# Second layer of a two-layer network: softplus pieces on ScalarE and direct products on VectorE stand at other steps

## The chip, the cores and the metric

The kernel runs on one core of one Trainium2 chip. Its engines are TensorE (PE; PEld is its weight load), VectorE (DVE), ScalarE (ACT), GpSimd (POOL) and SyncE (SP, which issues the DMAs). Each engine works through its own queue in order and waits for others through semaphores. The metric is device time in microseconds; before the change it is 8841.8 us, the median of three runs (8837.53 to 8855.01).

## The reference, cut to what matters

Everything is float32. The first layer is an attention block on 16 images of 128 channels and 56 x 56 pixels; the change leaves it alone. The second layer is a 3 x 3 convolution, a small state-space scan over 8 tokens, GroupNorm and a SiLU with residual:

```python
y = conv(x, conv_w) + conv_b
seq = y.reshape(B * H * W, 8, 16)                      # 8 tokens of 16 values a pixel
xi, z = split(seq @ in_proj_w.T)                       # 32 and 32
xc = silu(causal_conv1d(xi) + conv1d_b)
dt, Bm, Cm = split(xc @ x_proj_w.T, [1, 17])
dt = softplus(dt * dt_proj_w + dt_proj_b)
h = exp(dt * A) * h + dt * Bm * xc                     # for each of 8 tokens, 32 x 16 states
ym = (sum(h * Cm) + D * xc) * silu(z)
out = ym @ out_proj_w.T
return x + silu(groupnorm(out))
```

softplus(v) is computed as max(v, 0) + ln(1 + exp(-|v|)), with a correction of the rounding in 1 + e: u = (1 + e) - 1, and e - u is added to the logarithm.

## The kernel before, in words

The second layer (`layer1`) starts some 3250 us into the span. The work is cut into groups of 448 columns, 7 to an image, 112 in all. A group's scan runs in 14 steps, two a token (`jp` 0 and 1: each step takes half of the states, a tile of 128 x 896). The order of each engine's queue is written out by hand: the loop at the end of `layer1` runs over groups i and steps k, issues the scan's own instructions and then what `work(i, k)` lists for VectorE, TensorE and GpSimd (in this order). `_chain` keeps the recorded order on each engine. A list named `pe` holds steps that begin with a matmul, but what they issue on ScalarE goes into ScalarE's queue at the same place.

In each step k of group i stand, in this order:

- `advance` (VectorE): L946 multiplies the decay `a` (in PSUM, two buffers) by the state of the token before, L947 adds it to this token's input; for the last token, steps 12 and 13, L944 does it in one.
- `inject` (VectorE): L936 makes the input `h` of four steps later (at steps 10 to 13 that of the next group) from `x` (PSUM, one buffer) and the gate `bb`. The tiles `h` have four buffers; one that is written at step 12 for the next group was last read by GpSimd's weighing of token 5.
- `decay` (TensorE): L918 makes the exponent of step k + 2; `spread` (TensorE): L929 makes the `x` that L936 of step k + 1 reads.
- `decay_exp` (ScalarE): L921, the exponential of `a` in place, that L946 of step k + 2 reads.
- `weigh` (GpSimd, odd steps): L951 multiplies the states of a token by the gate `cb`.

`work(i, k)` adds the rest. For the next group (`nxt`) it prepares: `rate` (steps 1 and 2, one a half h): matmul L850 into bank `pq0`, then on ScalarE Abs L851 and Relu L852; `rate_exp`: L856 and L857 on ScalarE; `rate_log`: L861 and L862 on ScalarE; `rate_sum` (steps 6 and 8): L867 to L870 on GpSimd, which end with `dt` and `dtx`; `gate` (step 3): matmuls L876 into `pq0` and `pq1`, the copies L880 to `bs` and `cs` on ScalarE, and DMAs L882 to DRAM; `bring`: the loads of `bb` and `cb` from there; `inner(..., "zs", ...)` (step 4): matmuls L836, SiLU L837; `product` (step 10): L896 on GpSimd; `direct` (step 13): matmul L900 of that product into `pq0`. For the group after next, `sequences` (step 11: transposes L829 and copy L831) and `inner(..., "xc", ...)` (step 12). Each `inner` takes a ScalarE table load (L837), two SiLU, and a load back (L145): this is the SiLU burst that stands in steps 4 and 12.

For the group itself (`p`): `direct_mul`, L905 on VectorE, reads `pq0` that `direct` filled and `dtx`, and writes `ud`; `skip` (L966) and `gather` (L960, four matmuls) collect the token sums in `pq1`; `collect` (L973) adds `ud`; `gated` (L976) multiplies by `zs`; `project_out` (L994, with copies L1002, L1005 and L1007 on ScalarE) follows in steps 5 and 6 of the next group. The convolution of the next image (L787, into `pq0`) is spread over steps 5 to 10.

In the second group of an image the statistics of the image before are finished: L1027 with copy L1028, and L1038 with Ln L1039 and Exp L1040, through `pq0`. At step 12 of that group ScalarE also runs the normalising SiLU L1061 (`normalise`), two of 128 x 1568 with table loads, and GpSimd adds the residual (L1068) there and in the third group.

Of the kernel before, what the change touches and what calls it, by code (L numbers as in the profile page):

```python
# [711 lines left out]
def layer1(ctx: ExitStack, tc: tile.TileContext, x1, t, out):  # L712
# [45 lines left out]
    for w, name in ((wx, "b_kx"), (wv, "b_dtw")):  # L758
        k = w1.tile(list(w.shape), F32, tag="fold", name=name)
# [17 lines left out]
    def load_image(b):  # L777
        nc.sync.dma_start(pad[:, 1 : H + 1, 1 : W + 1], x1[b].rearrange("c (h w) -> c h w", w=W))
        tails[b] = w2.tile([P, 64], F32, tag="tail", name=f"tail_{b}")
# [104 lines left out]
    def bring(p, k, tokens):  # L884
        n = len(tokens)
        tile_ = w3.tile([P, 2, BLK], F32, tag="bc"[k] + "b", name=f"{'bc'[k]}b_{p['n']}_{tokens[0]}")
        src = p["dram", k][:, tokens[0] : tokens[0] + n, :].rearrange("s l n -> s (l n)")
        nc.sync.dma_start(
            tile_[:, 0:n, :].rearrange("p l n -> p (l n)"), src.unsqueeze(1).to_broadcast([16, 8, n * BLK])
        )  # L890
        for i, l in enumerate(tokens):
            p["gate", k, l] = tile_[:, i, :]
# [157 lines left out]
    def residual(b, k):  # L1050
        res = norms[b, k] = w1.tile([P, half], F32, tag="res", name=f"res_{b}_{k}")
        nc.sync.dma_start(res[0:64], x1[b][0:64, k * half : (k + 1) * half])
        if k == 0:
            nc.sync.dma_start(res[64:P], x1[b][64:P, 64 : half + 64])
        else:
            nc.sync.dma_start(res[64:P, 0 : half - 64], x1[b][64:P, half + 64 : HW])
            nc.sync.dma_start(res[64:P, half - 64 : half], x1[b][64:P, 0:64])
# [19 lines left out]
    def work(i, k):  # L1077


        def at(n):  # L1080
            return groups[n] if 0 <= n < len(groups) else None

        p, nxt, far, prev = at(i), at(i + 1), at(i + 2), at(i - 1)
        pe, dve, pool = [], [], []

        if prev:
            if k == 0:
                pe += [partial(gather, prev, 5), partial(gather, prev, 6)]
            if k == 1:
                pe.append(partial(gather, prev, 7))  # L1090
            if k == 3:
                dve.append(partial(collect, prev, 1))
            if k == 4:
                pool.append(partial(gated, prev, 1))
            if k in (5, 6):
                pe.append(partial(project_out, prev, k - 5))
            b = prev["b"]
            if prev["g"] % 2 and k in (9, 10):
                dve.append(partial(statistics, b, prev["g"] - 10 + k))
            if prev["g"] == NBLK - 1:  # L1100
                if k == 9:
                    dve.append(partial(statistics, b, NBLK - 1))
                if k == 12:
                    residual(b, 0)
        two = at(i - 2)
        if two and two["g"] == NBLK - 1:
            b = two["b"]
            if k == 3:
                pool.append(partial(deviation, b))
            if k == 5:  # L1110
                pe.insert(0, partial(group_var, b, 0))
            if k == 8:
                pool.append(partial(affine, b))
            if k == 12:
                pe += [partial(normalise, b, 0), partial(normalise, b, 1)]
            if k == 13:
                pool += [partial(store, b, 0, 0), partial(store, b, 0, 1), partial(residual, b, 1)]
        three = at(i - 3)
        if three and three["g"] == NBLK - 1 and k in (2, 4):
            pool.append(partial(store, three["b"], 1, k // 2 - 1))  # L1120

        if p:
            if k == 1:
                dve.append(partial(direct_mul, p))
            if k == 7:
                pe.append(partial(skip, p, 0))
            if k in (8, 9, 10):
                pe.append(partial(gather, p, k - 7))
            if k == 12:
                dve.append(partial(collect, p, 0))  # L1130
            if k == 13:
                pe += [partial(skip, p, 1), partial(gather, p, 4)]
                pool.append(partial(gated, p, 0))
            if k in (2, 6):
                bring(p, 0, {2: (4, 5), 6: (6,)}[k])
            if k in (1, 5, 9):
                bring(p, 1, {1: (3, 4), 5: (5, 6), 9: (7,)}[k])

        if nxt:
            if k in (1, 2):  # L1140
                pe.append(partial(rate, nxt, k - 1))
            if k in (2, 3):
                pe.append(partial(rate_exp, nxt, k - 2))
            if k in (3, 4):
                pe.append(partial(rate_log, nxt, k - 3))
            if k in (6, 8):
                pool.append(partial(rate_sum, nxt, k // 2 - 3))
            if k == 3:
                pe += [partial(gate, nxt, 0), partial(gate, nxt, 1)]
            if k == 4:  # L1150
                pe.insert(0, partial(inner, nxt, "zs", wz, w2, 0.0))
            if k == 7:
                bring(nxt, 0, (0, 1))
            if k == 8:
                bring(nxt, 1, (1, 2))
            if k == 11:
                bring(nxt, 0, (2, 3))
            if k == 10:
                pool.append(partial(product, nxt))
            if k == 13:  # L1160
                pe.append(partial(direct, nxt))

        if p and k in (5, 6, 7, 8, 9, 10) and p["b"] + 1 < NB:
            taps = {5: (0,), 6: (1,), 7: (2, 3), 8: (4, 5), 9: (6, 7), 10: (8,)}[k]
            pe.append(partial(convolve, p["b"] + 1, p["g"], taps))
        if p and p["g"] == NBLK - 1 and k == 11 and p["b"] + 2 < NB:
            load_image(p["b"] + 2)
        if two and two["g"] == NBLK - 1 and k == 2:
            pe.append(partial(group_mean, two["b"], 0))
        if far:  # L1170
            if k == 11:
                pe.append(partial(sequences, far))
            if k == 12:
                pe.insert(0, partial(inner, far, "xc", wx, w3, c1_b))
        return pe, dve, pool
# [16 lines left out]
    for i in range(-2, len(groups) + 3):  # L1192
        for k in range(14):
            now = 0 <= i < len(groups)
            if now:
                advance(*state_step(i, k))
            inputs = input_step(i, k + 4) if now or (i == -1 and k >= 10) else None
            if inputs:
                inject(*inputs)
            decays = state_step(i, k + 2) if now or (i == -1 and k >= 12) else None  # L1200
            if decays:
                decay(*decays)
            inputs = input_step(i, k + 5) if now or (i == -1 and k >= 9) else None
            if inputs:
                spread(*inputs)
            if decays:
                decay_exp(*decays)
            if now and k % 2:
                weigh(groups[i], 1 + k // 2)
            pe, dve, pool = work(i, k)  # L1210
            for part in (dve, pe, pool):
                for step in part:
                    step()
# [37 lines left out]
```

## Time and profile before

| | us |
|---|---|
| median of 3 runs | 8841.8 |
| the profiled execution, device time | 8843.74 |
| its span, first to last instruction | 8841.9 |
| L951 POOL, weigh, mean of 784 | 3.996 |
| L921 ACT, exponential, mean of 1568 | 0.900 |
| L936, L946, L947 DVE, means | 1.083, 1.091, 1.092 |
| L905 DVE, direct product, mean (4000 to 7000 us) | 0.676 |
| L856, L857, L861, L862 ACT, means (4000 to 7000 us) | 0.567, 0.578, 0.661, 0.561 |
| L837 and L145 ACT, table load | 1.283 |
| mean granted clock | 0.966 |

In the profile a line such as `6240.30 1.10 DVE L946 ... x1 [0.76 <-ACT a L921]` is read: at 6240.30 us of the span VectorE starts an instruction of line 946 that takes 1.10 us; before it the engine was idle for 0.76 us, and what ended the wait was ScalarE's line 921. A float32 matmul shows as several records (x2, x4, x8), and successive instructions of an engine overlap by some 0.1 us.

### The profile page before, as it was taken

To read this page: it belongs to the slowest core of one execution; us is meant where nothing else is said; L and a number is where in the kernel's file an instruction comes from. 1 tells how busy PE (TensorE), PEld (TensorE's weight loads), DVE (VectorE), ACT (ScalarE), POOL (GpSimd) and SP (SyncE) were. 2 spreads that over 40 slices of the span, in tenths; PEclk is the share of its full clock that TensorE was granted. 3 is DMA by queue.
4 is the path that set the end of the run, shared out by engine and by line. 5 is a ranking of instruction groups with operands and counts; after the bars stand their busy time and mean duration, and the time that the engine had idled before them with its cause. 6 is when DMAs were issued, how large, how long until landed. Compare 5 with 4: busy or idle time off the path is not lost.

```text
span 8841.9 us, 151450 instructions
## 1 busy us (share of the span) xinstructions
PE 8013.1 (91%) x52860; PEld 3322.9 (38%) x52860; DVE 7764.8 (88%) x10358; ACT 5603.8 (63%) x10516; POOL 7035.4 (80%) x5664
## 2 busy tenths in 40 slices
PE   6999999999999879999999999999999999999987
PEld 3444444444444433333333333333333333333332
DVE  7999999999999839898898988988988989889887
ACT  4776777777777636666655665665656665666654
POOL 5878888878888328888888888888888888888887
PEclk8999999999999989999999999999999999999997
DMA  2333333333333222333333333333333333333332
GB/s 62 85 85 89 87 87 87 86 87 89 87 86 88 76 61 80 93 90 83 90 90 83 91 83 99 84 88 93 87 85 86 88 92 91 82 98 85 87 89 69
DMA packets 764424, 757.86 MB, mean 86 GB/s; under 512 B 188688, under 2 KB 663952, under 8 KB 761616
## 3 DMA queue, kind: packets, MB, share of 16 engines
q1 hardware_dynamic: 763664, 748.18, 32.8%
q8 instruction: 422, 6.91, 0.3%
q14 instruction: 338, 2.77, 0.1%
HBM read 439.61 MB, written 102.76 MB: 61 GB/s over the span
## 4 chain that ended last, share of the span: by engine, by line
PE 31%; ACT 24%; DVE 21%; POOL 11%; issue 10%; DMA 1%; SPq 0%; ACTq 0%; POOLq 0%; DVEq 0%
PE pq L787 8%; PE a L918 8%; ACT a L921 5%; DVE a L946 5%; DVE lepe L460 4%; DVE h L947 4%; POOL xh L263 4%; PE pq L960 4%; POOL e L379 4%; PE x L929 3%; ACT L837 3%; DVE h L936 3%; POOL tap L261 2%; ACT L145 2%; DVE sst L363 2%
## 5 line engine op out<-in xcount | busy, mean ns | idle before, releaser
L951 POOL TENSOR_TENSOR cst<-h,cb 128x1792 f32<-128x1792 f32 x784 | 3129.4, 3996 | 855.1 <-DVE h L947 580.4
L921 ACT ACTIVATE a<-a 128x896 f32<-128x896 f32 x1568 | 1404.3, 900 | 1772.7 <-PE x L929 1174.8
L936 DVE TENSOR_TENSOR h<-x,bb 128x896 f32<-128x896 f32 x1568 | 1697.6, 1083 | 276.9 <-PE x L929 145.6
L918 PE MATMUL a<-dt,adec 32*128 32x448 f32 x6272 | 1659.7, 606 | 214.4 <-DVE h L947 213.5
L946 DVE TENSOR_TENSOR a<-a,h 128x896 f32<-128x896 f32 x1344 | 1466.3, 1091 | 358.1 <-ACT a L921 357.5
L460 DVE SCALAR_TENSOR_TENSOR lepe<-vpad,lep,lepe 128x448 f32<-128x448 f32 x2688 | 1718.4, 678 | 0.6
L929 PE MATMUL x<-dtx,amask 32*128 32x448 f32 x6272 | 1664.8, 608 | 25.5 <-DVE h L936 24.5
L947 DVE TENSOR_TENSOR h<-a,h 128x896 f32<-128x896 f32 x1344 | 1467.0, 1092 | 45.8
L379 POOL TENSOR_SCALAR e<-e,sst,zero 128x256 f32<-128x256 f32 x1568 | 861.6, 560 | 451.4 <-DVE sst L375 396.6
L369 ACT ACTIVATE e<-ps,sst 128x256 f32<-128x256 f32 x1568 | 728.8, 469 | 544.5 <-DVE sst L363 493.6
L787 PE MATMUL pq<-x1pad,conv 128*128 128x448 f32 x2016 | 942.8, 580 | 59.5 <-ACT gst L1039 32.5
L918 PEld LDWEIGHTS a<-dt,adec 32*128 32x128 f32 x6272 | 484.2, 188 | 1247.4 <-DVE h L947 578.4
L263 POOL TENSOR_TENSOR xh<-xh,tap 128x448 f32<-128x448 f32 x735 | 841.4, 1145 | 42.5
L960 PE MATMUL pq<-cst,sel 128*32 128x448 f32 x6272 | 750.9, 564 | 1.5 <-POOL cst L951 1.5
L401 PE MATMUL ptt<-ident,e 128*128 128x128 f32 x3136 | 546.4, 285 | 92.3 <-POOL e L379 75.2
L363 DVE TENSOR_REDUCE sst<-ps 128x2 f32<-128x512 f32 x784 | 540.4, 689 | 86.3 <-PE ps L357 63.8
L929 PEld LDWEIGHTS x<-dtx,amask 32*128 32x128 f32 x6272 | 485.0, 189 | 339.8 <-DVE h L936 333.7
L357 PE MATMUL ps<-sel,q 32*64 32x256 f32 x6272 | 540.8, 413 | 68.2 <-ACT e L369 61.7
L261 POOL TENSOR_SCALAR tap<-xpad,pos,zero 128x448 f32<-128x448 f32 x735 | 533.6, 726 | 34.4
L787 PEld LDWEIGHTS pq<-x1pad,conv 128*128 128x128 f32 x2016 | 349.2, 194 | 497.4 <-issue 441.9
L401 PEld LDWEIGHTS ptt<-ident,e 128*128 128x128 f32 x3136 | 367.9, 142 | 416.5 <-POOL e L379 238.0
L407 ACT COPY att<-ptt 128x512 f32<-128x512 f32 x784 | 458.6, 585 | 48.0 <-PE ptt L401 40.3
(164 smaller groups left out, 12292.7 us busy)
## 6 DMA issues: line engine op xcount, KB each, us to landing
sel<-kv SPq DMA_DIRECT2D x3136, 64.0 KB
bb<-db SPq DMA_DIRECT2D x336, 448.0 KB
cb<-dc SPq DMA_DIRECT2D x336, 448.0 KB
xpad<-x SPq DMA_DIRECT2D x32, 784.0 KB
x<-r SPq DMA_DIRECT2D x112, 224.0 KB
x1pad<-x SPq DMA_DIRECT2D x16, 1568.0 KB
db<-bs SPq DMA_DIRECT2D x112, 224.0 KB
dc<-cs SPq DMA_DIRECT2D x112, 224.0 KB
```

Source lines behind the costliest of these rows:

```text
L263: nc.gpsimd.tensor_add(im["xh"][i], im["xh"][i], held["tap"])
L379: nc.gpsimd.tensor_scalar(e, e, im["st", w][:, 2, p : p + 1], zero, ALU.mult, ALU.add)
L460: nc.vector.scalar_tensor_tensor(out, src, lep[:, k : k + 1], acc, ALU.mult, ALU.add)
L787: nc.tensor.matmul(pc, lhsT=conv[:, k, :], rhs=pad[:, 8 * i + dy : 8 * i + dy + 8, dx : dx + W], start=(k == 0), stop=(k == 8),)
L918: nc.tensor.matmul(a[:, k, :], lhsT=adec[rows, l4, :], rhs=p["dt"][rows, h, :], start=True, stop=True)
L921: nc.scalar.activation(p["a", l, jp], p["a", l, jp], AF.Exp)
L929: nc.tensor.matmul(x[:, k, :], lhsT=mask[rows, l4, :], rhs=p["dtx"][rows, h, :], start=True, stop=True)
L936: nc.vector.tensor_mul(p["h", l][:, own(jp), :], px["x"], weight)
L946: nc.vector.tensor_mul(a, a, before)
L947: nc.vector.tensor_add(p["h", l][:, own(jp), :], a, p["h", l][:, own(jp), :])
L951: nc.gpsimd.tensor_mul(c, p["h", l], p["gate", 1, l].unsqueeze(1).to_broadcast([P, 4, BLK]))
L960: nc.tensor.matmul(py[32 * j : 32 * j + 32], lhsT=sel[:, l4, :], rhs=p["c", l][:, j, :], start=False, stop=(l % 4 == 3), skip_group_check= ...
```

## The change

The direct products `direct_mul` move from step 1 to step 0. In step 13 the matmul `direct` goes ahead of `skip` and `gather` (with no group in work it stays where it was). The softplus pieces move: `rate_exp` of the second half from step 3 to step 6, `rate_log` of the first half from step 3 to step 5, and of the second half from step 4 to step 7. `rate_exp` of the first half stays in step 2.

```diff
         if p:
-            if k == 1:
+            if k == 0:
                 dve.append(partial(direct_mul, p))
...
             if k == 13:
+                if nxt:
+                    pe.append(partial(direct, nxt))
                 pe += [partial(skip, p, 1), partial(gather, p, 4)]
                 pool.append(partial(gated, p, 0))
...
         if nxt:
             if k in (1, 2):
                 pe.append(partial(rate, nxt, k - 1))
-            if k in (2, 3):
-                pe.append(partial(rate_exp, nxt, k - 2))
-            if k in (3, 4):
-                pe.append(partial(rate_log, nxt, k - 3))
+            if k in (2, 6):
+                pe.append(partial(rate_exp, nxt, k // 4))
+            if k in (5, 7):
+                pe.append(partial(rate_log, nxt, k // 2 - 2))
             if k in (6, 8):
                 pool.append(partial(rate_sum, nxt, k // 2 - 3))
...
-            if k == 13:
+            if k == 13 and not p:
                 pe.append(partial(direct, nxt))
```

## The prediction

> **What bounds the kernel now.** I read the page's shares, then the waits of the second layer, then the timeline of one group. Times such as "24.05" below are microseconds after that group's first L946, which starts at 6236.32 us of the span.
>
> The page, part 1:
> ```profile
> PE 8013.1 (91%) x52860; PEld 3322.9 (38%) x52860; DVE 7764.8 (88%) x10358; ACT 5603.8 (63%) x10516; POOL 7035.4 (80%) x5664
> ```
> The waits from 4000 to 7000 us, some 60 groups (total, times, longest):
> ```profile
> DVE a L946 <- ACT a L921: 199.1, 125, 6.6
> ```
> The windows view of the group (length, then PE, PEld, DVE, ACT and POOL busy):
> ```profile
> 6236.30:6283.90 47.60, 45.23 (x236) 16.15 (x235) 44.70 (x47) 29.45 (x42) 40.27 (x19) 1.00 0.29 78
> ```
> DVE is busy 44.7 of 47.6 us and has 2.9 us of holes; the waits say that ScalarE's exponential L921 ends most of them, twice a group. PE's 45.2 us can shrink: where L918 and L929 come up together they overlap (both done in 0.96 us), else they take 2.0. So DVE sets the pace, with PE and POOL close behind.
>
> The timeline around steps 0 and 1:
> ```profile
> 6238.46 1.08 DVE L936 TENSOR_TENSOR h<-x,bb 128x896 f32<-128x896 f32 x1
> ...
> 6239.36 0.90 ACT L921 ACTIVATE a<-a 128x896 f32<-128x896 f32 x1
> ...
> 6239.94 1.02 PE L900 MATMUL pq<-cs,cbm 128*128 128x448 f32 x2
> 6240.30 1.10 DVE L946 TENSOR_TENSOR a<-a,h 128x896 f32<-128x896 f32 x1 [0.76 <-ACT a L921]
> ...
> 6243.44 1.27 DVE L905 SCALAR_TENSOR_TENSOR ud<-pq,vec,dtx 128x448 f32<-128x448 f32 x2
> ```
> L946 of step 1 waits 0.76 us for an exponential held up by the first SiLU burst; the direct products L905, which need nothing from it, run after it. Around steps 4 to 7:
> ```profile
> 6254.62 0.56 ACT L862 ACTIVATE ln<-e 128x448 f32<-128x448 f32 x1
> ...
> 6256.86 1.28 ACT L837 ACT_TABLE_LOAD   x1
> ...
> 6259.15 1.28 ACT L145 ACT_TABLE_LOAD   x1
> ...
> 6260.44 0.67 ACT L861 ACTIVATE u<-u,neg 128x448 f32<-128x448 f32 x1
> 6260.94 1.13 POOL L867 TENSOR_TENSOR u<-u,e 128x448 f32<-128x448 f32 x1
> ...
> 6261.48 1.70 ACT L921 ACTIVATE a<-a 128x896 f32<-128x896 f32 x2
> 6262.41 1.10 DVE L946 TENSOR_TENSOR a<-a,h 128x896 f32<-128x896 f32 x1 [1.53 <-ACT a L921]
> ```
> Six softplus pieces (L856, L857, L861, L862 ahead of the copies L880 and the exponential, then L861 and L862 behind) sit around the second burst (load, two SiLU, load), and L946 of step 7 waits 1.53 us. Start to start, counted over all middle groups: step 0 takes 3.92 us in an ordinary group and step 6 4.75, against 3.13 for a plain step. So the two stalls cost 0.79 and 1.62 us.
>
> There are 112 groups, seven to an image: 15 second ones (51.6 us on average, with the group statistics of the image before), 15 third ones (58.7 us, behind that image's normalisation) and 82 others (47.54 us; the first image's second and third have nothing before them and count here).
>
> **The change, part by part.** No instruction is added or removed; DVE, PE, ACT and POOL have the same work in another order.
>
> *Direct products to step 0.* PE: L900 now goes ahead of skip L966 and gather L960. It needs the first SiLU half (done at 1.20) and product L896 (done four microseconds before this group began). So it runs 1.30 to 2.32; today PE sits idle 0.48 us there. Skip and gather follow, and the whole row ends at 4.1 instead of 4.57. DVE: L936 ends at 3.21, L905 then takes 2 x 0.59 = 1.18 us start to start, and L946 of step 1 starts at 4.30, not 3.97 (its exponential is done at 3.94). Step 2 starts at 7.45, not 8.30: 0.85 gained. Behind L905 stand L946, L947, L936 of step 1 and with them PE's L918 and L929; PE reaches those at 6.7 and 7.6 (today both 7.2). First rate product L850 goes from 9.09 to 9.57 and is the only one later; the second goes from 12.52 to 11.9. That loss is covered by PE's wait of 0.46 us on L947 right behind it.
>
> *Softplus away from the burst.* Out of ACT's queue before the copies L880 go L856, L857, L861, L862 (2.35 us); out of the place between the second load and the next exponential go L861 and L862 (1.05 us). What is late next: L880 can start at 16.1, not 18.77. But matmul L836 stands behind L918 and L929 of step 4, which wait for DVE, so it starts at 18.48 against 19.33. And the first load waits for its first half, as this line of a third group shows:
> ```profile
> 6158.18 1.28 ACT L837 ACT_TABLE_LOAD   x1 [0.43 <-PE pq L836]
> ```
> So load 19.5, SiLU 20.8, second load 21.8, exponential 23.1 to 24.0 (today 25.16 to 26.06). DVE would be ready for L946 of step 7 at 23.63, so 0.4 us of the stall stays and step 7 starts at 24.06, not 26.09. Of these 2.03 us, 0.85 are the first part's and 1.18 this one's. PE follows: project L994 no longer waits for zs, L966 of step 7 goes from 30.3 to 28.3, and the convolution stretch behind it, where PE has no hole, moves as a block.
>
> The pieces put back: L861 and L862 follow the exponential in step 5 (24.0 to 25.1), L856 and L857 stand behind the copies L1002 and L1005 in step 6, L861 and L862 behind the exponential of step 7 (28.8 to 30.0). Exponentials behind them are ready 1.4 to 2 us before DVE wants them; if that cover went, each late microsecond would be a stall. No moved piece issues a DMA, and SP's queue keeps its order; copies bs and cs are 2.7 us sooner, and with them SP's two stores L882 and the bb loads behind them.
>
> *POOL pays.* L867 starts today at 24.61, when POOL is free. Now POOL would be free at 23.8 but u is done at 24.65, so L867 starts at 24.7: POOL's chain (4.7 softplus, 4.0 weigh, 4.7, 4.0) ends its fifth weigh L951 at 42.1, as today. L936 of step 12 writes the h buffer that this weigh reads, the tile having four buffers: today it starts at 44.07 with 2.0 us in hand; now it would like to start at 41.85 to 42.05. So it waits till 42.2. From there to the next group nothing changes (3.54 us): a group takes 42.2 + 3.54 = 45.74 us, and this holds for the even and the odd groups, which are then all tied to POOL. Ordinary groups gain 47.54 - 45.74 = 1.8 us: 82 x 1.8 = 148.
>
> *Second groups.* The statistics' matmul and Ln (L1038, L1039) sit behind the same exponential and PE waits for them:
> ```profile
> 5060.80 1.46 PE L787 MATMUL pq<-x1pad,conv 128*128 128x448 f32 x2 [2.32 <-ACT gst L1039]
> ```
> With the exponential 2 us sooner I get a PE wait of 1.4 us, no stall over 0.4 at steps 7 to 11 (today 3.7 at step 7), and 47.3 us: gain 4.3, x 15 = 65. After that wait the windows view shows a granted clock of 0.50 from 5062.5 to 5064.5, and matmuls ran slow (L787 1.46, L918 1.12 a pair for 0.65); with the shorter wait I take them as fast. If the clock still fell, L787, L918 and L929 would cost 1.6 us more, 24 us in all. [...]
>
> *Third groups.* The 6.7 us stall at step 1 is the normalisation's, and PE, after 4.9 us of idling, then runs at a granted clock of 0.54 and is the bound to step 4, so L905 gains nothing there. Copies bs 2.1 us sooner bring the bb load, which DVE awaits for 2.4 us in step 8, 2.0 sooner: 15 x 2 = 30. Bounds: 0 (POOL holds SP) to 5 (all three stalls go).
>
> Sum: 148 + 65 + 30 = 243. The profiled execution took 8843.7 us (span 8841.9 and 1.8 around it), 1.9 above the median of 8841.8. 8843.7 - 243 = 8601, and against the median 8599: I say **8600**.
>
> **Rivals.**
> *POOL is later than I think.* For it: POOL has no hole from step 5 to step 13. If u is late by another 1 us, the loop is 46.7: 82 x 0.8 + 15 x 3.3 + 15 x 2 = 145, 8697.
> *PE takes step 7's gain back.* For it: L936 of step 12 already waits for L929 (0.2 to 0.8 us). Against: PE's block starts earlier too. Then step 0's part remains: 82 x 0.79 + 15 x 3 = 110, 8732.
> *Slower.* A DVE without stalls frees h and x at even intervals, so L918 and L929, which overlap when both wait for the same late DVE, come apart: 2.0 us of PE for 0.96. PE is busy 45.2 us a group; over 47.54 it would be with 2.3 more pairs apart. With three, 48.35: 97 x 0.8 = 78 us more, 8920. For it: pairs are apart today in steps 2, 3, 4 and 7, those where PE waits for DVE. Against: a PE that falls behind finds both ready and they overlap again; in my walk it is still four.
> *The change does nothing.* If L946 of step 1 waits at L905 instead (L900 held up beyond 3.1) and POOL eats the rest: within 0.2%.
> *Better.* If the h buffer never binds and third groups gain 4: 82 x 2.05 + 65 + 60 = 293, 8549.
>
> **How the numbers follow.** My forecast 0.60 (8560 to 8650), better 0.10, POOL later 0.14, PE 0.07, nothing 0.03, slower 0.06. The range 8530 to 8705 takes in the better case and the first rival and leaves out PE's, nothing and slower, with some of the first. Its measurement can tell about 0.2% (18 us): faster 0.91, same 0.03, slower 0.06.
>
> **What would show it.** L905 should stand before the second L946 of a group, with no wait on L921 there in ordinary groups; the wait at step 7 should be under 0.6; total of L946 on L921 should fall from 199 to some 80 (what is left is the third groups'). L867 should wait on ACT u L861 for about 0.9 us, and L936 should begin to wait for POOL cst L951. If L946 still waits over 1 us at step 7, the burst did not move; if L936 waits for L929 in steps 8 to 12 by more than today, PE took it.

## The result, and the profile after

The changed kernel takes 8619.4 us, the median of four runs (8605.7 to 8637.8), beside 8841.6 for the kernel before on the same chip: a ratio of 0.9747, with a 95% interval of 0.9726 to 0.9769. The forecast was 8600 in a range of 8530 to 8705. The profiled execution is the longest of the four (8637.8 us, span 8634.2).

The page of the changed kernel, part 1:
```profile
PE 7989.8 (93%) x52860; PEld 3357.5 (39%) x52860; DVE 7749.2 (90%) x10358; ACT 5624.3 (65%) x10516; POOL 7027.0 (81%) x5664
```
The same instructions in the same counts and, within 0.5%, the same busy times on PE, DVE, ACT and POOL: what went is idle time. The waits from 4000 to 7000 us of the changed kernel (total, times, longest) say which:
```profile
DVE a L946 <- ACT a L921: 69.5, 72, 5.5
...
POOL u L867 <- ACT u L861: 61.4, 66, 1.4
ACT L837 <- PE pq L836: 60.8, 63, 1.4
...
DVE h L936 <- PE x L929: 59.0, 76, 2.2
...
DVE h L936 <- POOL cst L951: 35.7, 50, 1.4
...
DVE h L936 <- DMA bb<-db: 28.7, 9, 4.3
```
The exponential's share fell from 199 to 70. Four waits have come or grown: GpSimd on u, the table load on matmul L836 (3.9 before), L936 on GpSimd's weigh, and L936 on the load of bb (17.2 before, in third groups). The one on the weigh is the new limit of an ordinary group. One such group begins at 6114.42 us; its windows view:
```profile
6114.40:6160.10 45.70, 45.05 (x236) 16.45 (x235) 44.61 (x47) 29.56 (x42) 40.15 (x19) 1.00 0.30 81
```
45.7 us instead of 47.6, with PE and DVE as busy as before. Its timeline on VectorE around steps 0 and 1:
```profile
6116.55 1.08 DVE L936 TENSOR_TENSOR h<-x,bb 128x896 f32<-128x896 f32 x1
6117.55 1.26 DVE L905 SCALAR_TENSOR_TENSOR ud<-pq,vec,dtx 128x448 f32<-128x448 f32 x2
6118.73 1.09 DVE L946 TENSOR_TENSOR a<-a,h 128x896 f32<-128x896 f32 x1
```
L905 stands before the group's second L946, and no bracket with a wait is left. ScalarE and VectorE around steps 4 to 7:
```profile
6133.96 1.28 ACT L837 ACT_TABLE_LOAD   x1 [1.08 <-PE pq L836]
...
6136.25 1.28 ACT L145 ACT_TABLE_LOAD   x1
...
6138.48 1.10 DVE L946 TENSOR_TENSOR a<-a,h 128x896 f32<-128x896 f32 x1 [0.36 <-ACT a L921]
```
ScalarE stands idle 1.08 us before the burst, till the first half of L836 is there, and L946 of step 7 waits 0.36 us for what follows the burst. Then GpSimd and step 12:
```profile
6139.10 1.14 POOL L867 TENSOR_TENSOR u<-u,e 128x448 f32<-128x448 f32 x1 [0.59 <-ACT u L861]
...
6152.55 4.00 POOL L951 TENSOR_TENSOR cst<-h,cb 128x1792 f32<-128x1792 f32 x1
```
```profile
6156.58 1.09 DVE L936 TENSOR_TENSOR h<-x,bb 128x896 f32<-128x896 f32 x1 [0.31 <-POOL cst L951]
```
GpSimd starts its softplus late because u is late, runs from there without a hole, and its fifth weigh ends at 6156.55, when L936 may write the buffer.

The lengths of the groups, first L946 to first L946, added up from the two profiled executions (81 ordinary, 15 second, 15 third):

| us | before | changed | gain | forecast |
|---|---|---|---|---|
| ordinary, all (each) | 3856.5 (47.61) | 3701.0 (45.69) | 155.5 | 148 |
| second, all (each) | 768.8 (51.25) | 725.2 (48.35) | 43.6 | 65 |
| third, all (each) | 879.3 (58.62) | 864.9 (57.66) | 14.4 | 30 |
| sum | | | 213.5 | 243 |

Second and third groups gave 37 us less than forecast, ordinary ones 7.5 more. The first layer, whose code is the same, took 6.8 us longer in the changed kernel's profiled execution; the medians are 222 apart.

### The profile page after: what moved, and what is told of

Same layout as the page of the kernel before. It is cut to its first block, busy times and chain, and to the rows that moved or that the text cites. A ratio compares the mean times of both kernels' runs of the same rounds, so it can differ in the third digit from the quotient of the medians.

```text
span 8634.2 us, 151465 instructions
## 1 busy us (share of the span) xinstructions
PE 7989.8 (93%) x52860; PEld 3357.5 (39%) x52860; DVE 7749.2 (90%) x10358; ACT 5624.3 (65%) x10516; POOL 7027.0 (81%) x5664
## 4 chain that ended last, share of the span: by engine, by line
PE 27%; DVE 25%; POOL 23%; ACT 12%; issue 11%; DMA 2%; POOLq 0%; SPq 0%; ACTq 0%; DVEq 0%
PE a L918 6%; DVE a L946 5%; DVE h L936 5%; POOL xh L263 5%; POOL cst L951 4%; PE x L929 4%; POOL e L379 4%; DVE lepe L460 4%; DVE h L947 4%; PE pq L787 3%; POOL tap L261 3%; PE pq L960 3%; PE pq L876 2%; POOL dtx L870 2%; DVE sst L363 2%
## 5 line engine op out<-in xcount | busy, mean ns | idle before, releaser
L951 POOL TENSOR_TENSOR cst<-h,cb 128x1792 f32<-128x1792 f32 x784 | 3126.9, 3994 | 549.6 <-DVE h L947 434.5
L936 DVE TENSOR_TENSOR h<-x,bb 128x896 f32<-128x896 f32 x1568 | 1695.7, 1081 | 317.4 <-PE x L929 205.9
L929 PE MATMUL x<-dtx,amask 32*128 32x448 f32 x6272 | 1658.6, 606 | 43.4 <-DVE h L936 35.9
L946 DVE TENSOR_TENSOR a<-a,h 128x896 f32<-128x896 f32 x1344 | 1463.1, 1089 | 118.2 <-ACT a L921 118.2
L947 DVE TENSOR_TENSOR h<-a,h 128x896 f32<-128x896 f32 x1344 | 1467.1, 1092 | 46.2
L929 PEld LDWEIGHTS x<-dtx,amask 32*128 32x128 f32 x6272 | 483.5, 188 | 360.4 <-DVE h L936 346.5
```

The costliest lines, as they stand in the source:

```text
L929: nc.tensor.matmul(x[:, k, :], lhsT=mask[rows, l4, :], rhs=p["dtx"][rows, h, :], start=True, stop=True)
L936: nc.vector.tensor_mul(p["h", l][:, own(jp), :], px["x"], weight)
L946: nc.vector.tensor_mul(a, a, before)
L947: nc.vector.tensor_add(p["h", l][:, own(jp), :], a, p["h", l][:, own(jp), :])
L951: nc.gpsimd.tensor_mul(c, p["h", l], p["gate", 1, l].unsqueeze(1).to_broadcast([P, 4, BLK]))
```

## The experiments

The theory: (a) the direct products free the 0.8 us of step 1; (b) the softplus pieces free 1.2 us at step 7, and 0.4 stay because the table load waits for matmul L836; (c) GpSimd's chain, which starts when u is there, then sets the length of an ordinary group through L936 of step 12; (d) what second and third groups gave less than forecast went to waits of TensorE and the falls of its clock behind them. The rivals stand in the expectations. All times are medians, ratios are to the kernel before (8842 to 8850 us beside them).

**One part alone.** The direct products, without the softplus pieces:
```diff
-            if k in (2, 6):
-                pe.append(partial(rate_exp, nxt, k // 4))
-            if k in (5, 7):
-                pe.append(partial(rate_log, nxt, k // 2 - 2))
+            if k in (2, 3):
+                pe.append(partial(rate_exp, nxt, k - 2))
+            if k in (3, 4):
+                pe.append(partial(rate_log, nxt, k - 3))
```


> Only the direct products and their matmul are moved; the softplus pieces stand where they stood before. Theory (the two stalls are separate, each hidden by its own part): the stall of 0.76 us at step 1 goes, the one of 1.5 at step 7 stays or grows by up to 0.25, since ScalarE's work ahead of the second burst comes only 0.6 sooner. An ordinary group 46.7 to 46.95 us, 8760 to 8785 us in all, no wait of L936 on POOL cst L951 at step 12. Rival (the burst has its own clock, DVE only arrives earlier at the same exponential): the step 7 stall grows by 0.8 and the time stays at 8842.

Measured: 8773.5, ratio 0.9914 (0.9899 to 0.9930). The stall of step 1 is gone, that of step 7 is 1.65 us in ordinary groups, which take 46.9. As the theory has it. By the profiles second groups gain 17.8 us in all and third ones lose 10.7, which the theory does not name.

The softplus pieces, without the direct products (`direct_mul` in step 1, `direct` behind `gather`):


> Only the softplus pieces are moved; the direct products stay in step 1. Theory: step 1 keeps its 0.76 us, the stall at step 7 falls to 0.4; L867 starts 0.9 later and the fifth weigh ends near 42.95, so L936 of step 12 waits on it for 0.1 to 0.2. An ordinary group 46.4 to 46.6, 8690 to 8720 us. Rival (the parts need each other: without the earlier DVE the burst stays where it was): step 7 keeps over 1 us of stall and the time is above 8780.

Measured: 8690.6, ratio 0.9822 (0.9808 to 0.9835); ordinary groups take 46.4, step 7 waits 0.38 in them, step 1 still 0.5 to 0.8. L936 of step 12 waits 0.64 us for L951, where 0.1 to 0.2 was expected. The waits from 4000 to 7000 us, of the direct products alone and then of the softplus pieces alone:
```profile
DVE a L946 <- ACT a L921: 155.3, 76, 5.5
```
```profile
DVE a L946 <- ACT a L921: 112.1, 124, 6.6
...
DVE h L936 <- POOL cst L951: 35.8, 50, 1.4
```
The first has half the number of stalls, the second all of them but shorter, and only the second has the wait on L951: that comes from the softplus part. By the ratios the parts give 0.9% and 1.8%, together 2.5%: nearly a sum.

**The 0.4 us at step 7.** The SiLU table for zs gets a load of its own ahead of matmul L836 (lines behind it move by two):
```diff
+        if which == "zs":
+            _act_set(tc, "silu_and_others")
         for h in range(2):
             nc.tensor.matmul(pq[h][:, 0:BLK], lhsT=w[:, h, :], rhs=p["seq"], start=True, stop=True)
```


> As the changed kernel, but the SiLU table for zs is loaded by an instruction of its own ahead of matmul L836, so the load no longer waits for that matmul. Theory (the 0.4 us left at step 7 is the load waiting for L836's first half, and L867 is late by the same microsecond): the load starts at about 18.5 instead of 19.5, the step 7 stall goes, L867 starts 1 us sooner and L936 of step 12 waits under 0.1 for L951; an ordinary group 45.0 to 45.2, 8555 to 8580 us. Rival (POOL's own work fills the group): step 7's stall goes but reappears at step 12 as a wait on L951 or L929, an ordinary group 45.6 and 8605 to 8625 us.

Measured: 8547.4, ratio 0.9664 (0.9650 to 0.9677), better than the theory's band. ScalarE's timeline there:
```profile
6071.65 0.90 ACT L923 ACTIVATE a<-a 128x896 f32<-128x896 f32 x1 [0.48 <-PE a L920]
6072.57 1.28 ACT L145 ACT_TABLE_LOAD   x1
6073.86 1.02 ACT L839 ACTIVATE zs<-pq 128x448 f32<-128x448 f32 x2
```
The load follows the exponential at once and runs beside the matmul, where the changed kernel has 1.08 us of waiting. Step 7 waits no more; u's instruction starts 22.9 us after the group's first step where it was 23.9, so GpSimd is no longer late, and L936 of step 12 waits for L929 again in most groups. Ordinary groups take 45.05. Second groups fell too, from 48.35 to 46.75, which the band had not counted: half a microsecond each where the clock held (46.2 for 46.7), and no slow stretch behind step 4 longer than 3.4 us in any but the last, where the changed kernel had six of 10.2.

**GpSimd's chain.** If u sets GpSimd's start, the first half's logarithm may go back to step 3 without touching the burst's end:
```diff
-            if k in (5, 7):
-                pe.append(partial(rate_log, nxt, k // 2 - 2))
+            if k in (3, 7):
+                pe.append(partial(rate_log, nxt, k // 4))
```


> As the changed kernel, but the logarithm pieces of the first half (L861, L862) stand in step 3 again, ahead of the copies bs and cs. Theory (an ordinary group is tied to POOL through L867, and the burst starts when matmul L836 is done, so 1.2 us on ScalarE ahead of it are free): L867 no longer waits, L936 of step 12 no longer waits on L951, the stall at step 7 stays 0.4, an ordinary group 45.2 to 45.5 against 45.69, 8580 to 8605 us. Rival (what counts is the ScalarE time around the burst): the step 7 stall grows by about 1 us and the time is 8690 to 8720.

Measured: 8637.1, ratio 0.9766 (0.9749 to 0.9782): a miss for both. In the profile the mechanism is there (L936 of step 12 no longer waits for L951, step 7 stays at 0.37, ordinary groups 45.51 for 45.69, 14.5 us in all), but third groups are 7.3 us longer in all and second ones 1.5. In third groups the early pieces stand ahead of the copy bs, which on average starts 24.7 us after the group's first L946 for 23.9, and L936 of step 8 waits 3.85 us for the load of bb where it waited 3.13: 10.8 us over the fifteen. The profiled execution (8626.4) is shorter than the changed kernel's (8637.8), so the profiles do not show where the 18 us between the medians lie; the intervals overlap. This was taken up again below, with second and third groups quieted first.

**Second groups.** In the changed kernel they have two main lengths, 46.7 (seven) and 50.5 us (six); the other two take 47.7 and 47.2. TensorE's timeline around step 5 in one of 50.5 and in one of 46.7:
```profile
5320.60 1.86 PE L787 MATMUL pq<-x1pad,conv 128*128 128x448 f32 x2 [1.28 <-ACT gst L1039]
```
```profile
5990.05 1.02 PE L787 MATMUL pq<-x1pad,conv 128*128 128x448 f32 x2 [1.27 <-ACT gst L1039]
```
and the windows of the 10.2 us from there, in the same order (the granted clock is the figure after the five engines):
```profile
5319.80:5330.00 10.20, 9.40 (x29) 3.98 (x30) 5.94 (x7) 5.00 (x11) 8.58 (x6) 0.50 0.33 81
```
```profile
5989.20:5999.40 10.20, 9.35 (x51) 3.83 (x52) 9.69 (x10) 7.46 (x14) 8.58 (x6) 1.00 0.29 85
```
The wait is the same; in the first group the clock falls to half at 5319.78 us, 0.46 us into it, and TensorE does 29 matmul records in the time of 51; in the second it does not fall. To test whether this wait is what lets the clock fall, the convolution's first tap goes behind the next one's step:
```diff
             taps = {5: (0,), 6: (1,), 7: (2, 3), 8: (4, 5), 9: (6, 7), 10: (8,)}[k]
-            pe.append(partial(convolve, p["b"] + 1, p["g"], taps))
+            if two and two["g"] == NBLK - 1 and k < 7:
+                taps = () if k == 5 else (0, 1)
+            if taps:
+                pe.append(partial(convolve, p["b"] + 1, p["g"], taps))
```


> The changed kernel, but in the fifteen second groups the first product tap of the convolution goes from step 5 to step 6, beside the second; nothing is left out. In the changed kernel's profile these groups last 46.7 us where the granted clock holds and 50.5 us where it falls to 0.5 after the wait of step 5 (7 of 15). Theory (the wait of TensorE on the normalised tile in step 5 is what lets the clock fall): step 5 waits no more, the clock falls in no second group, all fifteen last 46 to 47.5, and the time is 20 to 35 us below the changed kernel, 8585 to 8600. Rival (TensorE is late there anyway, and the wait and the fall of the clock go to step 6 or 7): second groups keep their two lengths, 8615 to 8640.

Measured: 8586.2, ratio 0.9705 (0.9686 to 0.9723). Second groups last 46.7 to 46.9 but for one of 47.9 and the last of 47.2, and the clock falls at step 5 in none, though seven had a point of the clock's grid in the place where it falls with the wait (see the paragraph on the clock below). The theory stands for these groups, 22.3 us in all by the profiles; third groups, whose order is the same, are 17.1 us shorter in this profile too, with 175 us of slow clock in them for 215.

**Third groups.** SP's timeline and then VectorE's in a third group of the changed kernel:
```profile
6038.88 2.44 SPq L1073 DMA_DIRECT2D out<-xr  x1
6041.36 2.28 SPq L888 DMA_DIRECT2D cb<-dc  x1
6043.74 3.91 SPq L888 DMA_DIRECT2D bb<-db  x2
```
```profile
6051.34 1.09 DVE L936 TENSOR_TENSOR h<-x,bb 128x896 f32<-128x896 f32 x1 [3.42 <-DMA bb<-db]
```
The loads are issued behind the three stores of the output, and L936 of step 8 waits 3.42 us. In the kernel before, the load stood behind the same stores, as SP's timeline in the third group that begins at 6129.26 us shows:
```profile
6159.39 2.42 SPq L1073 DMA_DIRECT2D out<-xr  x1
...
6164.22 3.03 SPq L888 DMA_DIRECT2D bb<-db  x2
```
There it is issued 35.0 us after the group's start, in the group of the changed kernel above, which begins at 6012.52, after 31.2 us. The stores go into a function of their own, three steps later:
```diff
-        if k == q == 1:
-            xr = xrs[b]
-            nc.sync.dma_start(outv[b, 0], xr[0:64])
...
+    def send(b):
+        xr = xrs[b]
+        nc.sync.dma_start(outv[b, 0], xr[0:64])
...
+        if three and three["g"] == NBLK - 1 and k == 7:
+            pool.append(partial(send, three["b"]))
```


> The changed kernel, but in the fifteen third groups the three stores of the output are issued in step 7 and not in step 4, so that the load of the coefficients bb is not behind them in SP's queue; nothing is left out. Theory (the load is late because it stands behind the stores, and its wait at L936 of step 8 starves TensorE, whose clock then falls): the wait of step 8, some 3.2 us a group, goes, so does the slow stretch at 41 us, third groups go from 57.7 to 54 to 55.5, the time is 30 to 55 us below the changed kernel, 8565 to 8590. Rival (the load is late by itself, by its landing time or its buffer): the wait stays within 0.5 us of its 3.2, and the time is 8610 to 8640.

Measured: 8574.1, ratio 0.9692 (0.9674 to 0.9711). SP's timeline and VectorE's, same place:
```profile
5995.86 1.82 SPq L888 DMA_DIRECT2D bb<-db  x2
5997.78 0.54 SPq L1072 DMA_DIRECT2D out<-xr  x1
```
```profile
6005.55 1.08 DVE L936 TENSOR_TENSOR h<-x,bb 128x896 f32<-128x896 f32 x1
```
The load is ahead of the stores and no wait is left. Third groups take 53.1 instead of 57.7 in the profiles, less than the band's 54 to 55.5; the fall of the clock at 41 us after their start, which came behind that wait, is gone.

**The three edits together,** and those with the early logarithm:

> The changed kernel with three edits: the SiLU table for zs loaded by an instruction of its own ahead of matmul L836 (alone 8547.4), the convolution tap of second groups one step later, and the stores of third groups in step 7; nothing is left out. If the three are independent: the first is worth 72; the second is worth little behind it, since the second groups are at 46.75 with the first alone, some 5 to 10; the third some 40: 8490 to 8510. If the waits are the same wait seen from several places: 8530 to 8550.

> The kernel with the three edits, and the logarithm of the first half's softplus and its weigh back in step 3 (it alone gave 8637.1 on the changed kernel where 8580 to 8605 was expected, though ordinary groups got shorter by 0.2). Theory (the loss there was in second and third groups, by the fall of the clock, and these are quiet here): ordinary groups 0.1 to 0.2 shorter, 8 to 16 us below the kernel with three edits. Rival (the early logarithm makes the burst of softplus dearer or later): 5 to 30 us above it, with a stall in step 3 or 4 that the other does not have.

Measured: 8475.2 and 8473.8, ratios 0.9581 (0.9562 to 0.9599) and 0.9581 (0.9563 to 0.9600). The first beat its band: the three edits gave 72, 33 and 45 us alone and 144 together, so the waits are separate ones, and this version is faster than both kernels. The second is equal to it, against both the theory and the rival: with the table load, GpSimd is not late in ordinary groups (45.0 in both), so there is nothing to gain there; second groups got 12.1 us shorter in all and third ones 15.4 longer.

**The early logarithm and the change itself, with second and third groups quiet.** Tap and stores moved, no table load; then the early logarithm on top; then the same two edits on the kernel before:

> The changed kernel with the convolution tap of second groups in step 6 and the stores of third groups in step 7, without the table load; nothing is left out. Alone the two were worth 33 and 45 us. Theory (each takes away its own wait and its own fall of the clock): 8619 - 33 - 45 = 8541, 8525 to 8555; second groups 46 to 47, third groups 52 to 53.5. Rival (a fall of the clock taken away at one place comes back at the other): 8565 to 8590.

> That kernel with the first half's logarithm and its weigh back in step 3. Theory (on the changed kernel the gain of ordinary groups, some 0.2 x 81 = 16 us, was lost in second and third groups by the fall of the clock): with these quiet, 10 to 20 us below the kernel without it, ordinary groups 45.4 to 45.5, L936 of step 12 not waiting for L951. Rival (the early logarithm costs as much in these groups as it gains, whatever the clock does): within 6 us of it, or above.

> The kernel before with the same two edits (tap of second groups in step 6, stores of third groups in step 7) and with softplus and direct products where they were; nothing is left out. It gives what the change is worth with these waits gone. Theory (the ordinary groups carry the change: 155 of 214 us in the two profiles; the falls of the clock only blur the rest): 8720 to 8765, that is 190 to 220 above the changed kernel with the same edits, ordinary groups 47.5 to 47.7. Rival (much of the change's gain in second groups was the step from two slow stretches to one, which the tap gives here too): 8690 to 8720, under 180 above.

Measured: 8534.0 (0.9652, 0.9633 to 0.9671), 8498.3 (0.9615, 0.9596 to 0.9634) and 8736.2 (0.9883, 0.9864 to 0.9902). The two edits add up as expected. The early logarithm, now on quiet ground, gains 36 us, more than forecast: in the profiles 14.8 in ordinary groups (45.71 to 45.52) and 15.2 in second ones, where L936 of step 12 waits 2.1 us for L951 without it and 0.8 us (for L929) with it; another 7.1 lie in the first layer, whose code is the same. Third groups lose nothing here (788.8 us in all for 790.1), since the load of bb is ahead of the stores. So (c) holds, and the miss on the changed kernel was in the other groups; why its median came out as high as 8637 is not settled.

The change by itself is worth 8736.2 - 8534.0 = 202 us here; by the profiles 155.2 in ordinary groups, 20.8 in second ones, 29.5 in third ones.

## Why the prediction came out right, step by step

The measured times below are those of the group that begins at 6114.42 us.

- **Direct products.** Right. L905 was to end so that step 1 starts at 4.30 and step 2 at 7.45 after the group's first L946; measured 4.31 and 7.44.
- **The burst.** Right. First load 19.5, last exponential 23.1 to 24.0, step 7 at 24.06; measured 19.54, 23.13 to 24.03, 24.06. The 0.4 us that were to stay are there, from the cause given: the own table load took them away.
- **GpSimd pays.** Right. L867 at 24.7, fifth weigh done at 42.1, L936 at 42.2; measured 24.68, 42.13, 42.16. The group was forecast at 45.74 and takes 45.69. The early logarithm shows that it was u: without its delay the wait on L951 is gone.
- **Second groups.** The mechanism was right where the clock held (47.3 forecast, 46.7 measured), and the term of 65 was mis-sized, 43.6. The step that failed is "with the shorter wait I take them as fast", an assumption that no view of before had shown: the wait did shrink from 2.3 to 1.3 us, but in six groups the clock still fell in it for 10.2 us, which costs 50.5 - 46.7 = 3.8 us and not the 1.6 that I priced from three matmuls, and in a seventh for 3.4 us, which cost 1.0. That makes 24 us, the most that I had set for all fifteen: at 46.7 in every group the term would have been 768.8 - 15 x 46.7 = 68. With tap and stores moved on both sides the change is worth only 20.8 us in these groups: on the kernel before, the same two edits alone take 44.0 us off them, so most of what I forecast was there TensorE's wait in step 5 and the slow clock behind it. (The 51.6 us that I started from is 51.25 from first L946 to first L946, which is 5 of the 65.)
- **Third groups.** Forecast 2.0 each, got 1.0. "Copies bs 2.1 us sooner bring the bb load, which DVE awaits for 2.4 us in step 8, 2.0 sooner" held as far as it goes. On average over the fifteen, counted from the group's first L946, the copy came 2.3 us sooner (26.2 to 23.9), the first issue of the load as much (34.5 to 32.2), and L936 of step 8 started 2.2 sooner (41.8 to 39.5). Its wait still grew, from 2.5 to 3.1 us, because VectorE was ready 2.8 sooner.
  The step that failed is "15 x 2 = 30", which carries the 2 us unchanged to the end of the group: from L936 of step 8 on, a third group took 18.1 us where it had taken 16.9, by the clock. In both profiles, leaving out the last third group, this stretch takes 16.3 us where the clock holds in it, 17.4 where it falls for 3.4 us and 18.7 to 19.0 where it falls for 6.8. In the kernel before it fell in eight of the fourteen, for 3.4 us; in the changed kernel in all, in six for 3.4 and in eight for 6.8. With tap and stores moved on both sides the change gives its 29.5.
- **The rivals.** POOL later (46.7) did not come; PE taking step 7 back did not (PE's L929 is not what L936 of step 12 waits for in most ordinary groups); the pairs did not come apart: PE is busy 45.05 us in the group, 45.23 before.

**The clock.** After the TensorE wait of 1.28 us the clock fell to 0.50, after the one of 1.27 us it held at 1.00. What differed was the place: the changes of the granted clock in the trace's records lie on a grid of 3.413 us that stays the same through the second layer, and in the fourteen second groups ahead of the last one the clock fell wherever a point of it came 23.43 to 24.06 us after the group's start, 0.46 to 1.09 us after the wait begins (seven), and nowhere else (seven, with points at 22.18 to 23.36). The 42 such groups of three other profiles (stores moved, early logarithm, own table load) widen the range: there the clock fell in the 23 with a point 0.52 to 2.53 us after the wait begins, and in none of the 19 others (0.50 at most, or 2.60 and more).

Open: why the clock fell at some points of the grid and held at others (TensorE's busy time in the step before does not tell by itself: in the changed kernel the clock still held at the end of 7316.6 to 7320.0 us, which has 2.09 us of it, and fell at the end of 5316.4 to 5319.8, which has 2.92), and whether the changed kernel with only the early logarithm is slower than without it at all.

## What to carry to other kernels

Follow the moved work to the next engine that must wait for it, with start and end times, until a buffer or a queue stops it: the 0.4 us of the table load and GpSimd's 42.1 both came out of that walk, and with them the gain of ordinary groups, 155 of 213 us. Where a transfer is to come sooner, read the issuing queue for what stands ahead of the load. And the second groups, with a wait of TensorE in step 5, had no single length here (46.7 us with the clock at 1.00, 50.5 with 10.2 us of it at 0.50): price such a stage with and without a fall of the clock, or take the wait away before comparing kernels.

## What the runs showed of the hardware that was not expected

In the changed kernel's second layer a slow stretch of the clock lasts one, two or three steps of the grid (3.41, 6.83 or 10.24 us) up to the last group, which has one of 17.07 and one of 34.67 that runs past the end of the span; second groups with the same wait of 1.3 us differed by 3.8 us, by where the grid met them. Executions of one kernel differ too, why is not shown: of the four of the changed kernel, the longest (8637.8) has the lowest mean clock, 0.967, and the shortest (8605.7) the highest, 0.972. In the kernel with three edits and the early logarithm an image takes 324.27 us, 95.0 times 3.413: there all fourteen middle images are alike, as two third groups, one image apart, show in the windows view:
```profile
6253.60:6306.30 52.70, 46.77 (x233) 17.04 (x232) 44.78 (x47) 35.61 (x46) 46.83 (x23) 0.90 0.42 116
6577.80:6630.50 52.70, 46.77 (x234) 17.05 (x232) 44.77 (x47) 35.62 (x46) 46.88 (x23) 0.90 0.42 116
```
The grid meets these images at the same place each time, and every third group of them has 10.2 us at a clock of 0.50 (52.7 us each; 50.3 to 53.9 with 6.8 us of it in the kernel with three edits), which is where its 15 us went. In its last five images the kernel with three edits has the same period (324.27 to 324.35 us).

A table load that stands ahead of an activation waited for that activation's matmul: 1.08 us in the group above, 60.8 us between 4000 and 7000 us. Loaded by an instruction of its own, the table was there beforehand, and the kernel 72 us faster.
